# Paged attention on one core: row sums moved within the step, token sums kept across key heads, and the keys' norm applied inside Exp

## The chip, the cores and the metric

The kernel is one program on one core of one Trainium2 chip. The metric is the device time of one execution in microseconds (us), lower is better; a kernel is compared by the median of several executions. Five engines of the core work from their own queues of instructions: PE (matrix products; its weight loads are listed apart as PEld), DVE (vector work), ACT (activations and copies), POOL (vector work and gathers) and SP (which issues transfers). [...]

## What is computed

Four layers follow one another: a gated feed-forward net with low-rank adapters and a mixture of adapters (layer 0), a small adapter layer with a routed feed-forward (layer 1), paged attention with another adapter layer (layer 2), and a routed layer with a sparse adapter (layer 3). The change lies in layer 2's attention, which is, cut down (there are 8 sequences of 128 tokens here, 512 features, 32 query heads and 8 key heads of 128, and 512 cached keys per sequence):

```python
q, k, v = (einsum('bsd,ed->bse', x, W).reshape(b, s, heads, 128) for W in (Wq, Wk, Wv))
q = rope(q * rsqrt(mean(q * q) + EPS) * q_norm_w, pos)      # 32 heads
k = rope(k * rsqrt(mean(k * k) + EPS) * k_norm_w, pos)      # 8 heads
k_all = concatenate([k_cache[block_table], k])              # 512 + 128 keys
v_all = concatenate([v_cache[block_table], v])
scores = where(valid, einsum('bqhd,bkhd->bhqk', q, k_all) / sqrt(128), -1e30)
o = einsum('bhqk,bkhd->bqhd', softmax(scores), v_all)
y = einsum('bse,de->bsd', o, Wo)
```

## The kernel before, in words

The attention runs from about 300 to 1465 us of the profiled span. It is cut into 32 **steps**, `steps[n] = (qd, p)`: eight key heads `qd`, and within each four pairs `p` of sequences. Four steps with one key head are called a quarter here. Step n computes the scores, weights and mixed values of its two sequences (j = 0 and 1) for the four query heads that share the key head; the projection of step n+1 and the output product of step n-1 run within step n.

The helpers, with their lines:

- `tokens` (L910) takes the four blocks of x that a step projects (two sequences, two halves of the features) and lets `combine` (L900) form four sums and differences of them on DVE (L907, tile `xs`). They are the token side of a scheme that needs seven block products in place of eight. The blocks depend on p alone, and not on qd.
- `seven` (L915) makes those seven products on PE (L925), with copies on ACT (L933) and additions on DVE (L936, L937). It has a hook, `between`, called after the fourth product. `project` (L953) uses it for q, k and v of the next step; ACT copies one block of the result out (L973) and DVE adds and stores the other three (L968). `leave` (L1125) uses it for the output product; there DVE (L1135) and POOL (L1138, L1143) add into y.
- `rotate` (L986) multiplies q and k by the rotary tables, on POOL (L997) and DVE (L1001), while ACT sums their squares (L1008). `normed` (L1019) adds the crossed terms (L1025), takes square roots on ACT (L1023) and the reciprocal on DVE (L1026), and multiplies both q and k by it (L1029).
- `turn_cached` (L1032) transposes blocks of the gathered cache keys on DVE (L1038, tile `kt`) and sends them through memory (four writes at L1042, a read at L1045) to get keys with features on the partitions (`kT`). `turn` (L1048) transposes the new keys and q on PE (L1053, L1060).
- `weigh` (L1066) makes the scores `st`, five blocks of 128 keys by 512 queries, on PE, and ACT writes their exponentials to `pT` (L1074), with the mask as bias for the four cached blocks and a bias of 0.0 for the new keys.
- `added` (L1080) sums the five blocks of `pT` on DVE (L1085, tile `part`); `divisors` (L1088) multiplies `part` by ones on PE to add over the keys (L1094, tile `sum`), takes the reciprocal on DVE (L1100) and copies four pieces of it into `R` (L1102), which transfers spread over the partitions (L1104).
- `mix` (L1108) multiplies the weights by the values on PE (tile `av`), and DVE scales the product by `R` (L1116, tile `oT`). `outputs` (L1118) makes the four combinations of `oT` for the output product (L907, tile `os`).

`run` (L1176) lists the order of a step. A scheduler may move instructions among the engines' queues, except those that go through `kept` (L847): once the loop runs, these keep the order in which the program lists them. Most of DVE's work and `SP`'s transfers are pinned in this way; PE's products are not.

Products land in rotating buffers of the accumulator memory: a group of three with the tag `mm` (projection, output product, `sum`, transposes), three with `st`, two with `av`. A product waits until the tile that held the buffer before has been read.

In the trace of before, one step reads on PE as follows, from the output product on: `wo` products; three `st` of j = 1; one `av` block; two `st`; four `av` blocks (they finish j = 0); `sum` of j = 1; the transposes of k and q for the next step, with an `av` block of j = 1 between; five `st` of the next step's j = 0; four `av` blocks (they finish j = 1); `sum` of j = 0; the seven products of the projection; and again `wo`.

Of the kernel before, what the change touches and what calls it, by code (L numbers as in the profile page):

```python
# [28 lines left out]
NQ = 8  # L29
# [754 lines left out]
def attention(tc, a, x, ident, lens, kvrow, part, ww, wop, ypool, sums, rot, eps, psa, c2, chunks, mm):  # L784
# [59 lines left out]

    running = []

    def kept(i):  # L847
        return tc.keep_in_program_order(i) if running or i.ins.engine == pool.engine else i

    def pair(n):  # L850
        p = steps[n][1]
# [48 lines left out]
    def combine(t, a11, a12, a21, a22):  # L900
# [6 lines left out]
            kept(dve.tensor_tensor(o, l, r, op))  # L907
        return a11, a12, a22, s1, s2, s3, s4

    def tokens(n):  # L910
        b = 2 * steps[n][1]
        parts = [x[:, 2 * h : 2 * h + 2, (b + j) * P : (b + j + 1) * P] for j in range(2) for h in range(2)]
        S[n]["A"] = combine(wk.tile([P, 4, 2, P], F32, tag="xs", name=f"xs_{n}", bufs=1), *parts)

    def seven(A, B, name, u, two, out2, out4, c11, c12, c21, c22, between=lambda: None):  # L915

# [33 lines left out]
    def nothing(_):  # L950
        pass

    def project(n):  # L953

        q = wk.tile([P, 2, REP, HD], F32, tag="q", name=f"q_{n}", bufs=1)
        k = wk.tile([P, 2, 1, HD], F32, tag="k", name=f"k_{n}", bufs=1)

        def places(j, i):

            heads = q[:, j, 2 * i : 2 * i + 2, :].rearrange("p h d -> p (h d)")  # L960
            if i:
                return (heads, slice(0, HW)), (vals[n % 2 * 2 + j][:, 4, :], slice(HW, KW))
            return (heads, slice(HD, KW)), (k[:, j, 0, :], slice(0, HD))

        def put(j, i):
            def f(ps, u):
                for to, at in places(j, i):
                    dve.tensor_tensor(to, ps[:, at], u[:, at], ALU.add)  # L968
            return f

        def copied(ps):
            for to, at in places(0, 0):
                act.copy(to, ps[:, at])  # L973

        def two():
            p6 = psa.tile([P, KW], F32, tag="st", name=f"q_six_{n}", bufs=3)
            return p6, psa.tile([P, KW], F32, tag="mm", name=f"q_five_{n}", bufs=3), True

        seven(
            S[n]["A"], W[steps[n][0]].B, f"q_{n}",  # L980
            wk.tile([P, 3, KW], F32, tag="u", name=f"uq_{n}", bufs=1), two, nothing, nothing,
            copied, put(0, 1), put(1, 0), put(1, 1),
        )
        S[n].update(q=q, k=k)

# [33 lines left out]
    def normed(n):  # L1019
        s = S[n]  # L1020
        s["rest"]()
        rs = wk.tile([P, 2, REP + 1], F32, tag="rs", name=f"rs_{n}")
        kept(act.activation(rs, s["ssq"], AF.Sqrt, bias=eps, scale=1.0 / HD))  # L1023
        for r, u in (s["rk"], s["rq"]):
            kept(dve.tensor_tensor(r, r, u, ALU.add))  # L1025
        kept(dve.reciprocal(rs, rs))  # L1026
        for m, at, nh in (("k", REP, 1), ("q", 0, REP)):
            r = s["r" + m][0]
            dve.tensor_tensor(r, r, rs[:, :, at : at + nh].unsqueeze(3).to_broadcast([P, 2, nh, HD]), ALU.mult)  # L1029
# [36 lines left out]
    def weigh(n, j):  # L1066

        s = S[n]
        b = 2 * steps[n][1] + j
        pT = wk.tile([P, NC, REP, P], F32, tag="pT", name=f"pT_{n}_{j}")  # L1070
        for c in range(NC):
            ps = psa.tile([P, REP * P], F32, tag="st", name=f"st_{n}_{j}_{c}", bufs=3)
            mm(ps, s["kT"][:, c, 4 * j : 4 * j + 4, :] if c < 4 else s["kn"][:, j, :], s["qT"][j], True, True)
            act.activation(  # L1074
                pT[:, c, :, :].rearrange("p i t -> p (i t)"), ps, AF.Exp,
                bias=hide[:, b, c : c + 1] if c < 4 else 0.0,
            )
        return pT

# [81 lines left out]
    def begin():  # L1161
        weights(0)
        out_weights(0)
        gather(0, "k")
        turn_cached(0)
        gather(0, "v")
        gather(1, "k")
        W[0].factors()

    def first(n):  # L1170
        tokens(n)
        project(n)
        rotate(n)
        normed(n)

    def run(pool_, end, bank):  # L1176
# [379 lines left out]
def ending(tc, a, out, x, ident, bias3, experts, early, tile_of_w2, tile_of_aw, chunks, mm):  # L1556
# [23 lines left out]


    L3 = SimpleNamespace()
    yT = early.tile([P, DC, NT], F32, tag="yT", name="y2T")
    A2 = small("A2", [P, DC, 32], chunks(a["A2"]))
    LiT = small("LiT", [32, 8], a["LiT"])
    Li = small("Li", [8, 32], a["Li"])
# [29 lines left out]
        sp.dma_start(W["a"], chunks(a["AwT"]))  # L1616

    def turn(y2, b, bank):
        ps = bank("mm", [P, DC, P], f"y2T_{b}")
        for c in range(DC):  # L1620
            pe.transpose(ps[:, c, :], y2[:, b, c * P : (c + 1) * P], ident)
        (act.copy if b % 2 else dve.tensor_copy)(yT[:, :, b * P : (b + 1) * P], ps)

    def low(g, bank):

        ps = bank("mm", [P, P], f"z2_{g}")
        for c in range(DC):
            for j in range(HB):
                b = g * HB + j
                mmq(ps[slot(j), :], A2[:, c, :], yT[:, c, b * P : (b + 1) * P], c == 0, c == DC - 1)  # L1630
        dve.tensor_copy(zq[:, g, :], ps)

    def anchors(g, bank):
        ps = bank("mm", [P, 2, 16], f"hd_{g}")
        for i in range(2):
            t0 = (2 * g + i) * 2 * P
            for c in range(DC):
                mm(ps[:, i, :], yT[:, c, t0 + 1 : t0 + 2 * P : 2], WH[:, c, :], c == 0, c == DC - 1)
# [13 lines left out]
    def product(b, tag, bank):  # L1652

        ps = bank(tag, [P, DC, P], f"h_{b}")
        for o in range(DC):
            for c in range(DC):
                mmq(
                    ps[:, o, :], W["2"][:, c, o * P : (o + 1) * P], yT[:, c, b * P : (b + 1) * P],
                    o == 0 and c == 0, False,
                )  # L1660
        H[b] = ps
# [343 lines left out]
```

## Time and profile before

| | |
|---|---|
| three runs, median (lowest to highest) | 1640.6 us (1638.76 to 1641.55) |
| the profiled execution's own time | 1622.67 us |
| its span, first to last instruction | 1620.4 us (mean granted clock 0.990) |
| PE busy | 1568.4 us, 97% of the span |
| PE's weight loads busy | 955.7 us, 59% |
| DVE busy | 1074.9 us, 66% |
| POOL busy | 818.3 us, 50% |
| ACT busy | 564.7 us, 35% |

The profile describes one execution, in microseconds from the span's start. A group line gives a source line, an engine, an operation, what it writes and reads, its shape and count, then the busy time, the mean duration of one in nanoseconds, and the engine's idle time before the group with what ended that idle time. The timeline lists an engine's instructions in order of time: start, length, engine and line, and in square brackets the idle time before it and the releaser. The chain of work that ended last is followed back from the last instruction, at each point to whatever released it; what isn't on the chain had time to spare.

### The profile page before, as it was taken

How to read it: one execution, taken by the hardware profiler on the slowest of the kernel's cores; microseconds unless marked ns; L12 is line 12 of the kernel's file. 1: busy time of each engine (PE TensorE's matmuls, PEld its weight loads, DVE VectorE, ACT ScalarE, POOL GpSimd, SP SyncE). 2: the span in 40 equal slices, each digit the busy share in tenths (PEclk: the TensorE clock that was granted, in tenths of full speed). 3: DMA queues.
4: the chain of work that ended last, by engine and by line, in shares of the span. 5: the costliest groups of instructions: out<-in, count | busy, mean ns of one | idle time of the engine just before them, and what ended most of it. 6: DMA issues, size and time to landing. Idle time of an engine off the chain costs nothing.

```text
span 1620.4 us, 19220 instructions
## 1 busy us (share of the span) xinstructions
PE 1568.4 (97%) x6305; PEld 955.7 (59%) x6305; DVE 1074.9 (66%) x2235; ACT 564.7 (35%) x1390; POOL 818.3 (50%) x778
## 2 busy tenths in 40 slices
PE   9999998979999999999999999999999999999998
PEld 7888884445555555555555555555555555559653
DVE  4575523477878787787878777787787877743141
ACT  1111110244445544444544444544444553420210
POOL 1341107254666676666667666666765676710000
PEclk9999998999999999999999999999999999999899
DMA  9110003031323323232332223323232332311000
GB/s 299 38 41 23 1 1 103 34 116 53 111 67 102 116 69 100 68 111 75 102 106 75 94 74 104 90 88 110 71 99 71 111 100 65 122 31 64 0 20 35
DMA packets 92237, 127.98 MB, mean 79 GB/s; under 512 B 19360, under 2 KB 59488, under 8 KB 92000
## 3 DMA queue, kind: packets, MB, share of 16 engines
q1 hardware_dynamic: 73984, 89.65, 17.9%
q0 software_dynamic: 17056, 36.49, 7.5%
q8 instruction: 52, 0.85, 0.2%
q10 hardware_dynamic: 1088, 0.52, 0.1%
q14 instruction: 57, 0.47, 0.1%
HBM read 92.91 MB, written 21.10 MB: 70 GB/s over the span
## 4 chain that ended last, share of the span: by engine, by line
PE 77%; DVE 15%; POOL 3%; DMA 2%; issue 2%; ACT 1%; SPq 0%; ACTq 0%; DVEq 0%; POOLq 0%
PE st L53 10%; PE av L53 10%; PE q_six L925 8%; PE g L362 7%; PE q_one L925 5%; PE q_five L925 5%; PE wo_two L925 5%; PE dn L362 4%; DVE part L1085 4%; PE wo_one L925 3%; PE wo_six L925 3%; DVE rq L1025 3%; DVE xs L907 2%; PE z L53 2%; PE h L1574 2%
## 5 line engine op out<-in xcount | busy, mean ns | idle before, releaser
L893 POOL DMA_INDIRECT vals<-in_v_cache,kvrow_v x256 | 273.1, 1067 | 73.2 <-issue 52.1
L893 POOL DMA_INDIRECT kn<-in_k_cache,kvrow_k x256 | 267.0, 1043 | 79.9 <-issue 77.6
L53 PE MATMUL av<-pT,vals 128*128 128x512 f32 x640 | 296.2, 594 | 0.0
L53 PE MATMUL st<-qT,kT 128*128 128x512 f32 x512 | 239.1, 599 | 4.3 <-DMA kT<-turned 4.3
L53 PEld LDWEIGHTS av<-pT,vals 128*128 128x128 f32 x640 | 119.4, 191 | 137.8 <-issue 135.6
L1074 ACT ACTIVATE pT<-st,hide 128x512 f32<-128x512 f32 x256 | 169.5, 687 | 46.6 <-PE st L53 43.9
L997 POOL TENSOR_TENSOR vq<-q,txq 128x512 f32<-128x512 f32 x64 | 83.5, 1326 | 161.2 <-DVE q L968 161.2
L53 PEld LDWEIGHTS st<-qT,kT 128*128 128x128 f32 x512 | 93.6, 192 | 99.4 <-issue 80.0
L1085 DVE TENSOR_TENSOR part<-pT 128x512 f32<-128x512 f32 x128 | 85.5, 692 | 68.6 <-ACT pT L1074 68.6
L1143 POOL TENSOR_TENSOR y<-y,uo 128x512 f32<-128x512 f32 x32 | 44.1, 1379 | 115.3 <-DVE y L1135 115.3
L1062 ACT COPY qT<-qTp 128x512 f32<-128x512 f32 x64 | 37.5, 586 | 169.2 <-PE qTp L1060 169.2
L925 PE MATMUL q_one<-q,x 128*128 128x384 f32 x256 | 96.2, 498 | 0.0
L925 PE MATMUL q_six<-q_s,xs 128*128 128x384 f32 x256 | 94.3, 486 | 0.0
L1008 ACT ACTIVATE sqq<-q 128x128 f32<-128x128 f32 x256 | 79.4, 310 | 8.3 <-DVE q L968 1.5
L1116 DVE TENSOR_TENSOR oT<-av,R 128x512 f32<-128x512 f32 x64 | 44.1, 688 | 42.5 <-PE av L53 39.1
L1025 DVE TENSOR_TENSOR rq<-rq,vq 128x1024 f32<-128x1024 f32 x32 | 70.4, 2200 | 1.2 <-POOL vq L997 1.2
L925 PEld LDWEIGHTS q_six<-q_s,xs 128*128 128x128 f32 x256 | 48.6, 190 | 36.1 <-issue 4.0
L1102 DVE COPY R<-r 32x128 f32<-32x128 f32 x256 | 66.1, 258 | 3.7
L925 PE MATMUL wo_one<-o,oT 128*128 128x256 f32 x256 | 65.8, 379 | 0.0
L933 ACT COPY uq<-q_one 128x384 f32<-128x384 f32 x32 | 15.3, 479 | 144.0 <-PE q_one L925 144.0
L53 PE MATMUL st<-qT,kTs 128*128 128x512 f32 x128 | 65.5, 593 | 0.0
L925 PEld LDWEIGHTS q_one<-q,x 128*128 128x128 f32 x256 | 46.0, 189 | 31.4 <-issue 6.0
(391 smaller groups left out, 2883.5 us busy)
## 6 DMA issues: line engine op xcount, KB each, us to landing
turned<-kt SPq DMA_DIRECT2D x128, 128.0 KB
kT<-turned SPq DMA_DIRECT2D x32, 512.0 KB
R<-R SPq DMA_DIRECT2D x192, 64.0 KB
q<-in_WqT SPq DMA_DIRECT2D x8, 1024.0 KB
o<-in_WoT SPq DMA_DIRECT2D x8, 1024.0 KB
kn<-in_k_cache,kvrow_k POOLq DMA_INDIRECT x256, 2.6
vals<-in_v_cache,kvrow_v POOLq DMA_INDIRECT x256, 2.7
wd<-in_WdT SPq DMA_DIRECT2D x2, 1280.0 KB
```

The source lines that it names most:

```text
L53: pe.matmul(o, lhsT, rhs, start=start, stop=stop)
L362: pe.matmul(o, lhsT, rhs, start=start, stop=stop, skip_group_check=True)
L893: kept(pool.indirect_dma_start(out=d[:, c, :], out_offset=None, in_=kc if what == "k" else vc, in_offset=bass.IndirectOffsetOnAxis(ap=kvro ...
L925: pe.matmul(o, l[:, c, :], r[:, c, :], start=start and c == 0, stop=c == 1, skip_group_check=True)
L997: kept(pool.tensor_tensor(u[:, :, :, lo : lo + 64], t[:, :, :, hi : hi + 64], wx[:, :, lo : lo + 64].unsqueeze(2).to_broadcast(part_), ALU ...
L1008: kept(act.activation(sq, t[:, j, i, :], AF.Square, accum_out=ssq[:, j, at + i : at + i + 1]))
L1025: kept(dve.tensor_tensor(r, r, u, ALU.add))
L1074: act.activation(pT[:, c, :, :].rearrange("p i t -> p (i t)"), ps, AF.Exp, bias=hide[:, b, c : c + 1] if c < 4 else 0.0,)
L1085: kept(dve.tensor_tensor(o, l, r, ALU.add))
L1102: kept(dve.tensor_copy(R[0:32, i * P : (i + 1) * P], r[32 * i : 32 * i + 32, :]))
L1116: kept(dve.tensor_tensor(S[n]["oT"][:, j].rearrange("p i t -> p (i t)"), ps, S[n]["R", j], ALU.mult))
L1143: kept(pool.tensor_tensor(t, t, u.unsqueeze(1).to_broadcast([P, 2, HW]), ALU.add))
```

## The change

Six things are edited.

1. **The row sums move.** `divisors(n, 0)` is called no longer right after `mix(n - 1, 1)` but through the hook `between` of the next step's projection. `divisors(n - 1, 1)` is called no longer at the end of its own step but in the next one, after the scores of j = 0.
2. **Token sums are kept.** For the key heads 1 to 6, `xs` of a pair p is computed once, in a tile that all of them share; heads 0 and 7 compute theirs anew as before. The shared tile takes the place that the last stage's transposed y (`y2T`) uses later, and `y2T` is therefore allocated when it is first written.
3. **The new keys are not multiplied by their norm.** The multiplication of k at L1029 is gone; the reciprocal root, one number for each key, becomes the scale of the Exp of the fifth block, where keys lie on the partitions.
4. **The turn of the cached keys moves** behind the output product and its additions, on DVE and on SP. Its DVE transposes are now always pinned.
5. **In `normed`** the additions are listed ahead of the square root, and the multiplication of q is pinned.
6. **At the start** `turn_cached(0)` moves from `begin` to behind the projection of step 0.

Built, the changed kernel has 47 rows of `xs` work on DVE in place of 127, and the 32 multiplications of k are gone. PE's order in a middle step is now: `wo` products; three `st` of j = 1; one `av` block; two `st`; four `av` blocks; the transposes; one `av` block of j = 1; **`sum` of j = 1**; three `av` blocks; five `st` of the next j = 0; the last `av` block; five of the projection's products and half of the sixth; **`sum` of j = 0**; the rest of the projection; and again `wo`. The `sum` of j = 0 takes over the buffer of the projection's first product (`q_one`). On DVE the reciprocal and the four copies of j = 0 stand among the projection's additions; the `kt` transposes stand after the last addition into y and ahead of the additions of the crossed terms.

```diff
-    def kept(i):
-        return tc.keep_in_program_order(i) if running or i.ins.engine == pool.engine else i
+    def kept(i, always=False):
+        return tc.keep_in_program_order(i) if always or running or i.ins.engine == pool.engine else i
...
+    kept_sums = {}
+
     def tokens(n):
-        b = 2 * steps[n][1]
+        qd, p = steps[n]
+        b = 2 * p
+        if 0 < qd < NQ - 1 and p in kept_sums:
+            S[n]["A"] = kept_sums[p]
+            return
         parts = [x[:, 2 * h : 2 * h + 2, (b + j) * P : (b + j + 1) * P] for j in range(2) for h in range(2)]
-        S[n]["A"] = combine(wk.tile([P, 4, 2, P], F32, tag="xs", name=f"xs_{n}", bufs=1), *parts)
+        if 0 < qd < NQ - 1:
+            if not kept_sums:
+                late.append(late[0].tile([P, NP, 4, 2, P], F32, tag="yT", name="xs_all"))
+            S[n]["A"] = kept_sums[p] = combine(late[1][:, p], *parts)
+        else:
+            S[n]["A"] = combine(wk.tile([P, 4, 2, P], F32, tag="xs", name=f"xs_{n}", bufs=1), *parts)
...
-    def project(n):
+    def project(n, between=lambda: None):
...
-            copied, put(0, 1), put(1, 0), put(1, 1),
+            copied, put(0, 1), put(1, 0), put(1, 1), between,
...
         rs = wk.tile([P, 2, REP + 1], F32, tag="rs", name=f"rs_{n}")
+        for m in "kq":
+            r, u = s["r" + m]
+            kept(dve.tensor_tensor(r, r, u, ALU.add))
+            s[m] = r
         kept(act.activation(rs, s["ssq"], AF.Sqrt, bias=eps, scale=1.0 / HD))
-        for r, u in (s["rk"], s["rq"]):
-            kept(dve.tensor_tensor(r, r, u, ALU.add))
         kept(dve.reciprocal(rs, rs))
-        for m, at, nh in (("k", REP, 1), ("q", 0, REP)):
-            r = s["r" + m][0]
-            dve.tensor_tensor(r, r, rs[:, :, at : at + nh].unsqueeze(3).to_broadcast([P, 2, nh, HD]), ALU.mult)
-            s[m] = r
+        full = [P, 2, REP, HD]
+        kept(dve.tensor_tensor(s["q"], s["q"], rs[:, :, 0:REP].unsqueeze(3).to_broadcast(full), ALU.mult))
+        s["rs"] = rs
...
             kept(dve.transpose(
                 t[:, :, 4 * j : 4 * j + 4, :], s["kc"][j].rearrange("p c (b d) -> p b c d", b=4)
-            ))
+            ), True)
...
                 pT[:, c, :, :].rearrange("p i t -> p (i t)"), ps, AF.Exp,
-                bias=hide[:, b, c : c + 1] if c < 4 else 0.0,
+                **(
+                    dict(bias=hide[:, b, c : c + 1]) if c < 4
+                    else dict(bias=0.0, scale=s["rs"][:, j, REP : REP + 1])
+                ),
...
         gather(0, "k")
-        turn_cached(0)
         gather(0, "v")
...
         project(n)
+        if n == 0:
+            turn_cached(n)
         rotate(n)
...
             pT = weigh(n, 0)
+            if last:
+                divisors(n - 1, 1)
             added(n, 0, pT)
             if last:
                 mix(n - 1, 1, last)
-            divisors(n, 0)
-            if last:
                 outputs(n - 1)
             if after:
-                project(after)
+                project(after, lambda: divisors(n, 0))
+                leave(n - 1, lambda: rotate(after))
+            else:
+                divisors(n, 0)
             if n + 1 < len(steps):
                 turn_cached(n + 1)
-            if after:
-                leave(n - 1, lambda: rotate(after))
-            elif last:
+            if last and not after:
                 leave(n - 1)
...
             mix(n, 0, pT)
-            divisors(n, 1)
             if n + 1 < len(steps):
                 turn(n + 1)
...
+        divisors(n, 1)
         mix(n, 1, last)
         outputs(n)
```

The remaining hunks replace the name of the last stage's `yT` by the tile allocated at its first use.

More of the change, by code (lines that the diff above doesn't have):

```diff
@@ L1582, in ending @@
     L3 = SimpleNamespace()
-    yT = early.tile([P, DC, NT], F32, tag="yT", name="y2T")
+    Y2T = []
     A2 = small("A2", [P, DC, 32], chunks(a["A2"]))
@@ L1618, in turn @@
     def turn(y2, b, bank):
+        if not Y2T:
+            Y2T.append(early.tile([P, DC, NT], F32, tag="yT", name="y2T"))
         ps = bank("mm", [P, DC, P], f"y2T_{b}")
@@ L1621, in turn @@
             pe.transpose(ps[:, c, :], y2[:, b, c * P : (c + 1) * P], ident)
-        (act.copy if b % 2 else dve.tensor_copy)(yT[:, :, b * P : (b + 1) * P], ps)
+        (act.copy if b % 2 else dve.tensor_copy)(Y2T[0][:, :, b * P : (b + 1) * P], ps)
     def low(g, bank):
@@ L1629, in low @@
                 b = g * HB + j
-                mmq(ps[slot(j), :], A2[:, c, :], yT[:, c, b * P : (b + 1) * P], c == 0, c == DC - 1)
+                mmq(ps[slot(j), :], A2[:, c, :], Y2T[0][:, c, b * P : (b + 1) * P], c == 0, c == DC - 1)
         dve.tensor_copy(zq[:, g, :], ps)
@@ L1637, in anchors @@
             for c in range(DC):
-                mm(ps[:, i, :], yT[:, c, t0 + 1 : t0 + 2 * P : 2], WH[:, c, :], c == 0, c == DC - 1)
+                mm(ps[:, i, :], Y2T[0][:, c, t0 + 1 : t0 + 2 * P : 2], WH[:, c, :], c == 0, c == DC - 1)
         dve.tensor_tensor(
@@ L1657, in product @@
                 mmq(
-                    ps[:, o, :], W["2"][:, c, o * P : (o + 1) * P], yT[:, c, b * P : (b + 1) * P],
+                    ps[:, o, :], W["2"][:, c, o * P : (o + 1) * P], Y2T[0][:, c, b * P : (b + 1) * P],
                     o == 0 and c == 0, False,
```

## The prediction, with its working

> **What bounds the kernel now.** I read the page first, then PE's waits, then the chain in order of time, then the timeline of one step. In the page, PE is busy nearly throughout, but DVE holds 15% of the chain:
>
> ```profile
> PE 1568.4 (97%) x6305; PEld 955.7 (59%) x6305; DVE 1074.9 (66%) x2235; ACT 564.7 (35%) x1390; POOL 818.3 (50%) x778
> PE 77%; DVE 15%; POOL 3%; DMA 2%; issue 2%; ACT 1%; SPq 0%; ACTq 0%; DVEq 0%; POOLq 0%
> ```
>
> Since no product is removed, only PE's waits can be won. Their list (us in total, times, longest) names what the change can touch:
>
> ```profile
> PE sum L1094 <- DVE part L1085: 19.2, 23, 2.6
> ...
> PE st L53 <- DMA kT<-turned: 4.3, 1, 4.3
> PE y2T L1621 <- POOL y L1143: 3.7, 2, 2.9
> PE eo_l L53 <- DVE x L300: 2.6, 1, 2.6
> ```
>
> The chain in one step shows how `sum` comes to wait: for about 10 us DVE alone carries it, from the crossed terms through k's and q's norm and the token sums to the sums of `pT`.
>
> ```profile
> 805.19 0.88 PE wo_six L925 x4
> 806.85 2.21 DVE rq L1025
> 809.22 0.70 DVE rk L1029
> 809.92 1.13 DVE rq L1029
> 811.43 1.10 DVE xs L907 x3
> 812.52 1.21 DVE part L1085 x2
> 813.76 0.70 DVE part L1085
> 814.56 0.70 DVE part L1085
> 816.53 0.86 PE av L53 x2
> ```
>
> The same view gives the step length as the distance between its rows of ten `st`: 35.17 us, but 34.43 from 538.00 to 572.43, the one step in four whose `xs` are not in this place.
>
> ```profile
> 502.83 4.29 PE st L53 x10
> 538.00 4.29 PE st L53 x10
> 572.43 4.29 PE st L53 x10
> 607.60 4.29 PE st L53 x10
> ```
>
> So the late `part` costs 0.74 us in three of four steps, and nothing in the fourth. In PE's timeline the pause ahead of `sum` in this step is 0.67 us.
>
> [...] the crossed-term addition of q, which lies beside POOL's additions into y (806.60 to 809.64 in its timeline), takes 2200 ns in the mean, the multiplication of the same size right after 1213 ns[...]. [...] Exp with the mask as bias takes 687 ns, with a constant 597 ns. [...] The trace has half-clock stretches of 3.41 us right after pauses of 4.3 us (at 363) and 2.6 us (at 1342).
>
> **The change part by part.** All sums are made against the profiled execution's own time, 1622.7 us (1620.4 span, 2.3 around it); the median of the runs is 1.0110 times that. Let S be the start of the first `st` of j = 1 (805.89 in the step shown) and T the start of `q_one`.
>
> *`sum` of j = 1 goes behind one more `av` block, k's norm and most `xs` go away.* Behind S, PE now has five `st` and five `av` blocks of 0.86 us, the transposes (0.28, 0.44, 0.44) and an `av` block (0.86): `sum` comes up at S + 10.6. On DVE, the last addition into y ends at S + 0.6; two `kt` transposes of 0.69 us follow, in place of nothing; then the additions of k (0.41) and q. POOL's additions into y end at S + 3.7 in the trace, so I let the contended addition end at S + 4.2, the reciprocal (0.20) and the multiplication of q (1.21) at S + 5.7, four `part` additions (2.75) at S + 8.5; with `xs` (1.5) at S + 10. Both are ahead of S + 10.6: the wait goes. [...] Of PE's 23 waits two are 2.6 and 1.7 us; one of 1.5 lies at 395, where weights are prepared on DVE; the other 20 are 0.67 to 0.74. Gain: 20 x 0.74 = 14.8, and 1.5 at 395. The removed DVE work, some 33 us of `xs` (80 x 417 ns) and 21.8 us of k's norm (32 x 681 ns), is worth nothing beyond these waits. Bounds: 10 to 17 together.
>
> *The norm as Exp's scale* makes 64 activations some 90 ns longer. PE's `st` and ACT's Exp run in turn at 0.86 us and 0.69: it is hidden. If ACT were late, 64 x 0.09 = 5.8 us is the most.
>
> *`sum` of j = 0 within the projection.* Its order needs the buffer of `q_one`, which ACT's two copies release. Before:
>
> ```profile
> 832.43 1.45 PE L925 MATMUL q_five<-q,xs 128*128 128x384 f32 x4
> 832.63 0.37 ACT L973 COPY q<-q_one 128x256 f32<-128x256 f32 x1 [4.64 <-PE q_one L925]
> 832.90 0.27 ACT L973 COPY k<-q_one 128x128 f32<-128x128 f32 x1
> ```
>
> The copies end at 833.17, or 0.74 after the fifth product begins; half of that product takes 0.65. With 0.06 for the semaphore (the reciprocal starts 0.08 after `sum` ends at 815.72) PE waits 0.15 in each of 29 steps: +4.4 (0 to 8.7, if it is none or twice that).
>
> On DVE, the reciprocal (0.95) and the four copies now stand ahead of the last additions of the projection:
>
> ```profile
> 826.24 0.95 DVE L1100 RECIPROCAL r<-sum 128x128 f32<-128x128 f32 x1
> 827.22 1.15 DVE L1102 COPY R<-r 32x128 f32<-32x128 f32 x4
> ```
>
> Five products of 1.29 (the first 0.1 more) and half of the sixth take until T + 7.2, so `sum` runs from T + 7.34 to 7.76, the reciprocal to 8.8, the addition of `q_five` to 9.2, the copies to 10.2, the addition that stores v to 10.4. `wo_one` can take the buffer of `sum`, free at 8.8. `wo_two` needs the one of `q_five`, at T + 10.6: 0.2 us to spare, cost nothing. The addition of `q_six` follows at 10.4 to 11.2, 0.4 to 0.6 us later against the output product than before, and POOL's rotary products with it; the crossed terms need them only at S + 2.3, some 2 us after they were ready before. `R`'s transfers get about 10 us more than before.
>
> *The turn of cached keys* leaves DVE's idle time. On SP its four writes (1.9 us of issue at 837.07) and read follow 5.8 us later; at 835.75 to 845 the way from the transposes to `kT` took 9 us beside weight transfers, so it lands at S + 10 at worst, and `st` needs it at S + 12. R's transfers stand ahead of it on SP and are long issued. Cost 0; 1 us a step if it were 3 us slower.
>
> *Late steps.* Of the 2.6 us at 1342, where POOL has an extra addition, I leave half, as the same chain on DVE is shortened by 2.2 and lengthened by 1.4; without a pause that long, the half-clock stretch behind it, worth 1.0, should go: -2.3 (0 to -3.6). The wait of `y2T` for POOL stays. At the end `sum` of the last j = 1 comes after the last Exp: +0.5.
>
> *Start.* The additions of x no longer stand behind q's crossed terms (-1.8 of 2.6); the projection now fills the wait for `kT` of step 1 (-4.3, and -1.6 for its half clock); against that, `sum` of step 0 waits some 3.6 in place of 1.7 and may bring a half-clock stretch (+1.9, +1.7), and the first `kT`, now queued on SP behind the 2 MB that are moved from 329 to 334, lands at about 335 to 336, when `st` needs it (336.34): +1.1. Together -3 (-6 to +3).
>
> Sum: -14.8 - 1.5 - 2.3 - 3.0 + 4.4 + 0.5 = -16.7, so 1606.0 in the profiled execution; times 1.0110, **1623.7**.
>
> **Rivals.** *Slower: DVE's queue inside the projection.* The reciprocal and copies, 2.1 us, stand ahead of the additions that free `wo_two`'s buffer, with 0.2 us to spare. If they run later than I have them, each step waits anew. Without the slot's 4.4 the gain is 21.1, so 0.73 us in 29 steps eats it all; at 1.0 us the profiled time is 1622.7 - 21.1 + 29 = 1630.6, or 1648.6. For it: the copies of one step can take 1.15 together, and everything after them is in one queue. Against: POOL is idle from 831.4 to 835.8[...].
> *Half the gain:* [...] -8, or 1632.5. Against it stands the 2 us of room in steps without `xs`.
> *More gain:* the slot's wait is hidden and the half-clock stretches at the start and at 1342 vanish: -14.8 - 1.5 - 3.6 - 6 + 0.5 = -25.4, or 1614.9.
> *The moves cancel:* waits merely go over to other products, within 0.2%.
>
> **Numbers.** As described 0.60 (own range 1618 to 1630), more gain 0.13, half the gain 0.12, no change 0.04, slower 0.11. A measurement can tell about 0.2% (3.3 us) from no change. Hence faster 0.85, same 0.04, slower 0.11. The range leaves out the slower case and the tail of the strong one: 1611 to 1637.
>
> **What would show it.** Right: steps of 34.4 to 34.7 us throughout; PE's wait `sum` on `part` under 4 us in all; `sum` of j = 0 waiting about 0.15 for ACT's copies; `wo_two` not waiting for DVE; the fifth Exp near 690 ns; no wait for `kT` at 363. Wrong: a new wait of `wo_two` or `rq`'s chain in each step; `kT` on the list with many entries; steps above 35.2.

## The result, and the profile after

The changed kernel took 1686.97 us in the median of four runs (1677.89 to 1693.08), the kernel before 1641.07 us (1638.76 to 1642.21) beside it: a ratio of 1.0277, with a 95% interval of 1.0229 to 1.0325. The forecast was 1623.7, faster.

The runs that followed fell on five chips, on two of which the kernel before took about 1624 us and on three 1644 to 1700 us, so each ratio below compares kernels on one chip, and the chip is named (that of this first result is not recorded).

The profiled execution of the changed kernel took 1686.06 us (span 1683.9, mean granted clock 0.979). Its page, with the row of busy times and the chain's shares by engine:

```profile
PE 1589.4 (94%) x6305; PEld 962.6 (57%) x6305; DVE 1012.7 (60%) x2123; ACT 565.7 (34%) x1388; POOL 798.6 (47%) x778
PE 85%; issue 3%; DVE 3%; DMA 2%; POOL 2%; another core or an unknown queue 2%; ACT 1%; SPq 0%; ACTq 0%; DVEq 0%; POOLq 0%
```

DVE's share of the chain fell from 15% to 3%, as the change intends, and yet the span is 63.5 us longer than in the profile of before. One entry has no place in a program on a single core: 2% of the chain were released by "another core or an unknown queue". PE's waits (us in total, times, longest):

```profile
PE q_five L938 <- DVE uq L950: 18.4, 10, 8.6
PE st L53 <- ACT pT L1089: 16.7, 3, 8.3
PE q_one L938 <- ACT uq L946: 14.9, 5, 3.1
PE sum L1112 <- ACT k L986: 13.6, 14, 1.3
PE y2T L1643 <- POOL y L1161: 3.8, 2, 3.0
PE sum L1112 <- DVE part L1103: 3.2, 2, 2.7
```

`sum` on `part`, 19.2 us before, is down to 3.2. Four waits have come up, and they are irregular: `q_five` waits 10 times among some 30 steps, `st` 3 times but for up to 8.3 us. The chain's rows of ten `st` show the same scatter:

```profile
541.54 4.29 PE st L53 x10
...
577.16 4.29 PE st L53 x10
...
613.00 4.29 PE st L53 x10
...
649.37 4.29 PE st L53 x10
```

These steps are 35.62, 35.84 and 36.37 us long; one, from 948.68 to 989.21, takes 40.53. In the profile of before, and in that of `after_fifth` below, the steps of the middle repeat in groups of four; here they do not.

One such wait, read in the timeline of all engines in the changed kernel (start, length, engine and line, and in brackets the idle time before it):

```profile
1068.20 1.45 PE L938 MATMUL q_five<-q_s,xs_all 128*128 128x384 f32 x4
...
1069.07 0.48 ACT L946 COPY uq<-q_one 128x384 f32<-128x384 f32 x1 [3.42 <-PE q_six L938]
...
1070.49 0.56 DVE L949 TENSOR_TENSOR uq<-q_six,uq 128x384 f32<-128x384 f32 x1 [1.21 <-PE q_five L938]
...
1070.66 0.94 POOL L893 DMA_INDIRECT kn<-in_k_cache,kvrow_k  x1 [0.30 <-issue]
1070.78 1.45 PE L938 MATMUL q_one<-q,x 128*128 128x384 f32 x4
1073.25 0.56 DVE L950 TENSOR_TENSOR uq<-q_five,uq 128x384 f32<-128x384 f32 x1 [2.20 <-PE q_one L938]
...
1073.86 0.91 PE L938 MATMUL q_five<-q,xs_all 128*128 128x384 f32 x2 [1.63 <-DVE uq L950]
```

The addition at L950 needs the product `q_five`, which ended at 1069.65, and the addition at L949, which ended at 1071.05. It starts at 1073.25, when no work that it needs is left, and PE stands for 1.63 us. What is late is PE's semaphore update: between 1070.40 and 1073.23 PE's semaphore has no record, although products with an update ended at 1070.94 and 1072.23 too. Until 1071.60, when the last one ends, POOL issues gathers.

### The profile page after: what moved, and what is told of

It reads as the page before. It is cut to its first block, busy times and chain, and to the rows that moved or that the text cites. A ratio compares the mean times of both kernels' runs of the same rounds, so it can differ in the third digit from the quotient of the medians.

```text
span 1683.9 us, 19213 instructions
## 1 busy us (share of the span) xinstructions
PE 1589.4 (94%) x6305; PEld 962.6 (57%) x6305; DVE 1012.7 (60%) x2123; ACT 565.7 (34%) x1388; POOL 798.6 (47%) x778
## 3 DMA queue, kind: packets, MB, share of 16 engines
q1 hardware_dynamic: 73984, 89.65, 17.6%
q0 software_dynamic: 17056, 36.49, 7.2%
HBM read 92.91 MB, written 21.10 MB: 68 GB/s over the span
## 4 chain that ended last, share of the span: by engine, by line
PE 85%; issue 3%; DVE 3%; DMA 2%; POOL 2%; another core or an unknown queue 2%; ACT 1%; SPq 0%; ACTq 0%; DVEq 0%; POOLq 0%
PE av L53 16%; PE st L53 15%; PE g L362 7%; PE q_six L938 7%; PE q_one L938 6%; PE q_five L938 5%; PE wo_two L938 5%; PE dn L362 4%; PE wo_one L938 3%; PE wo_six L938 3%; PE z L53 2%; PE h L1594 2%; PE o L53 2%; PE sum L1112 2%
## 5 line engine op out<-in xcount | busy, mean ns | idle before, releaser
L893 POOL DMA_INDIRECT vals<-in_v_cache,kvrow_v x256 | 283.3, 1107 | 73.3 <-issue 51.8
L893 POOL DMA_INDIRECT kn<-in_k_cache,kvrow_k x256 | 262.3, 1025 | 97.9 <-issue 76.1
L53 PE MATMUL av<-pT,vals 128*128 128x512 f32 x640 | 303.7, 601 | 0.0
L53 PE MATMUL st<-qT,kT 128*128 128x512 f32 x512 | 239.4, 598 | 16.7 <-ACT pT L1089 16.7
L1118 DVE RECIPROCAL r<-sum 128x128 f32<-128x128 f32 x64 | 61.2, 956 | 62.3 <-PE sum L1112 49.5
L938 PE MATMUL q_six<-q_s,xs_all 128*128 128x384 f32 x192 | 69.8, 486 | 0.0
L1120 DVE COPY R<-r 32x128 f32<-32x128 f32 x256 | 59.8, 234 | 3.7
L938 PE MATMUL wo_two<-o_s,os 128*128 128x256 f32 x256 | 60.6, 380 | 0.4 <-DVE vals L981 0.4
L986 ACT COPY q<-q_one 128x256 f32<-128x256 f32 x32 | 11.9, 373 | 145.8 <-PE q_one L938 136.9
```

The lines of the kernel that those rows point to most:

```text
L53: pe.matmul(o, lhsT, rhs, start=start, stop=stop)
L893: kept(pool.indirect_dma_start(out=d[:, c, :], out_offset=None, in_=kc if what == "k" else vc, in_offset=bass.IndirectOffsetOnAxis(ap=kvro ...
L938: pe.matmul(o, l[:, c, :], r[:, c, :], start=start and c == 0, stop=c == 1, skip_group_check=True)
L1118: kept(dve.reciprocal(r, ps))
L1120: kept(dve.tensor_copy(R[0:32, i * P : (i + 1) * P], r[32 * i : 32 * i + 32, :]))
```

## The experiments

Two theories were set against each other. *Parts*: one of the edits makes the new waits. *Late updates*: in some runs the semaphore updates of PE, ACT and DVE come late while POOL's gathers run; then it is a condition that the run meets, and the changed order merely pays more for it. To tell them apart in a trace, I counted for each engine the updates that have no record of their own within 0.12 us after the end of the instruction that makes them (late, or not recorded; these are called not prompt).

### Which part, and does the result repeat

The changed kernel unaltered (`same_again`), and the kernel before with one part each: kept token sums alone (`b_tokens`), row sums moved alone (`b_divs`), the turn of cached keys moved alone (`b_turn`).

```diff
# b_tokens
+        if 0 < qd < NQ - 1 and p in kept_sums:
+            S[n]["A"] = kept_sums[p]
+            return
# b_divs
+            if last:
+                divisors(n - 1, 1)
...
-                project(after)
+                project(after, lambda: divisors(n, 0))
...
-            divisors(n, 1)
# b_turn
-        turn_cached(0)
...
+            if n + 1 < len(steps):
+                turn_cached(n + 1)
```

> The changed kernel itself, unchanged, in a new load beside the kernel before. Theory A (semaphore updates of PE, ACT and DVE come late while POOL's gathers run, and the program's order brings that on): again about 1.02 to 1.03 times the kernel before, with 20 or more late updates in each step. Theory B (the late updates belong to one load or one session of the chip and not to the program): no late updates, and then what was predicted without them, about 0.99. Theory C (the row sum inside the projection simply waits for ACT's copies and DVE's queue, nothing is late): again 1.02 to 1.03, but with updates prompt, which the trace of the first run already speaks against.

> The kernel before with the kept token sums alone. All theories: in steps of the key heads 2 to 6 the 80 additions are gone from DVE and the wait of the row sum of j = 1 (0.74 us in three of four steps) goes with them, so some 10 to 15 us faster, ratio 0.991 to 0.994. Theory A, if the kept sums or the shared tile bring on the late updates: slower, 1.01 to 1.03, with late updates during the gathers.

> The kernel before with the two moves of the row sums alone. My working: the wait on part goes in 20 steps (-15 us), the slot of q_one costs 0.15 in 29 (+4), so 0.992 to 0.996 if updates are prompt. Theory C or theory A with the row sums as the cause: 1.01 to 1.03, in A with late updates during the gathers, in C without.

> The kernel before with the turn of the cached keys moved behind the output product, and at the start, alone. My working: 1.4 us more on DVE's chain ahead of part, so 1.4 us more waiting in some 28 steps at worst: 1.00 to 1.025, with prompt updates; theory A with this move as the cause: late updates during the gathers and ACT and DVE waiting for products long done.

Measured, all on chip 15 (before 1643.82 us): `same_again` 1690.77, ratio 1.0286 [1.0253, 1.0319]; `b_tokens` 1663.67, 1.0135 [1.0083, 1.0188]; `b_divs` 1716.76, 1.0445 [1.0409, 1.0481]; `b_turn` 1698.88, 1.0320 [1.0287, 1.0352]. So the slowdown repeats. `b_divs` lies above all that was expected for it, and every part that was tried alone is slower, even the kept sums, which only take away work of DVE and place the sums elsewhere. The parts do not add up either: 1.4, 4.5 and 3.2% make 9.0, all edits together 2.9%. That speaks against one guilty part. In all four traces several hundred updates are not prompt (the table below; `same_again` has 298 of DVE and 142 of ACT), and in the profile of before sixteen.

### The same before on another chip, and without gathers

`before_again` is the kernel before. `b_hw` and `a_hw` are the kernels before and after with the attention's gathers replaced by plain transfers that SP issues; they read fixed rows of the cache instead of those that the block table chooses, so their keys and values are other ones, of the same amount.

```diff
-                kept(pool.indirect_dma_start(
-                    out=d[:, c, :], out_offset=None, in_=kc if what == "k" else vc,
-                    in_offset=bass.IndirectOffsetOnAxis(ap=kvrow[what][:, qd, i : i + 1], axis=0),
-                ))
+            g0 = (2 * p + j) * 512 + qd * 64
+            src = (kc if what == "k" else vc)[g0 : g0 + 512, :].rearrange("(c p) d -> p c d", p=P)
+            kept(sp.dma_start(d[:, 0:4, :], src))
```

> The kernel before, unchanged, with a new profile. If late semaphore updates belong to the conditions of these timed runs and not to the change, this profile shows them too, during POOL's gathers, in about the number of the changed kernel (20 to 30 in a step), and the waits they bring add up to the 18 us between the profiled execution of the first page (1622.7) and the timed runs (1641). If they belong to the change, this profile is free of them as the first one was.

> The kernel before with the 512 indirect gathers of keys and values on POOL replaced by 128 plain transfers issued by SP, of rows that the block table does not choose (so the attention reads other keys and values). If late updates come with POOL's gathers, none is left and the time falls to about the span of the first page, 1620 to 1625, or ratio 0.985 to 0.99. If they come from something else, 1635 to 1650 with late updates.

> The changed kernel with the same replacement of the gathers. If my sum was right but for late updates, then with prompt updates this is 10 to 20 us faster than the kernel before with the replacement, 1600 to 1612, ratio 0.975 to 0.983. If the order of the change is at fault by itself (the row sum waiting for ACT's copies, DVE's queue in the projection), it stays slower than that kernel by 20 to 45 us: 1645 to 1670.

Measured on chip 1 (before 1623.58 us in the median of 23 runs): `before_again` 1623.26, ratio 1.0003 [0.9995, 1.0012]; `b_hw` 1611.07, 0.9929 [0.9910, 0.9948]; `a_hw` 1592.73, 0.9823 [0.9807, 0.9840]. Two things follow. The kernel before, which took 1641 to 1644 us elsewhere, takes 1624 here, so its first profile (1622.67) was no sample of the 1640.6 that stood beside it. And without gathers the change brings 18.3 us (1611.07 to 1592.73), about the 16.7 of the forecast. Both kernels came out below their ranges (1620 to 1625 and 1600 to 1612), because the replacement itself brings 12.5 us where updates are prompt (1623.58 to 1611.07), which no expectation had.

### The changed kernel and the row sums on a third chip

No edit (`after_third`), and the same edit as `b_divs` (`b_divs_second`).

> The changed kernel, unchanged, once more, since the kernel before took 1641 to 1644 us where updates were late and 1623 where they were prompt. Where the kernel before is at 1622 to 1625 here: theory A' (the change is worth what was worked out, and late updates during gathers turn it round) gives 1602 to 1610, ratio 0.987 to 0.992, with at most a handful of late updates. Theory D (the change by itself brings late updates) gives 1660 to 1695 with 20 or more late updates in a step. Where the kernel before is at 1640 or more: about 1688, as twice already.

> The two moves of the row sums alone, which cost 4.5% with late updates. With prompt updates: 20 waits on part of 0.74 go, 29 of 0.15 come, so 1610 to 1616, ratio 0.992 to 0.996. With late updates: 1710 to 1722 again.

Measured on chip 13 (before 1643.55 us): 1683.71, ratio 1.0268 [1.0224, 1.0312], and 1716.35, 1.0451 [1.0394, 1.0508]. Updates were late again (the table below), so this tells only that the result repeats on a further chip, for both kernels within 0.2%.

### A slow before, and the changed kernel without gathers beside it

No edit (`before_third`, `after_fourth`), and the edit of `a_hw` again (`a_hw_second`).

> The kernel before with a profile beside the changed one. Where it takes 1640 us or more I expect late updates during the gathers in this profile too (20 or more in a step), and fewer PE waits from them than in the changed kernel: some 18 us in all. Where it takes 1623, none.

> The changed kernel once more. Where the kernel before takes 1623 here: 1602 to 1610, ratio 0.987 to 0.992, updates prompt. Where it takes 1640 or more: 1680 to 1692, ratio 1.024 to 1.032, updates late. A time of 1680 beside 1623, or of 1605 beside 1641, would sink the theory that late updates decide the sign.

> The changed kernel with plain transfers by SP in place of the indirect gathers (it reads rows that the block table does not choose). If late updates come only while POOL gathers, this kernel has none here, whatever the kernel before takes, and stays at 1592 to 1597; beside a kernel before of 1643 that is a ratio of 0.97. If the condition makes updates late without gathers as well, it is 1620 or more.

Measured on chip 2 (before 1700.25 us): `before_third` 1699.13, ratio 0.9987 [0.9969, 1.0005]; `after_fourth` 1731.78, 1.0169 [1.0110, 1.0228]; `a_hw_second` 1593.50, 0.9365 [0.9315, 0.9416]. The expected sizes were missed: the kernel before was to lose some 18 us to late updates, and the changed one was to take 1680 to 1692. The last run is the strongest single result: on the chip where the kernel before loses 76 us, the changed kernel without the attention's gathers takes 1593.50, on chip 1 it took 1592.73. The condition was there in this execution: six gathers at the start of the program remain in it (6.3 to 15.1 us), and during these, or within 0.4 us behind them, seven updates of DVE are not prompt, against none in `a_hw` on chip 1. After them there is none on DVE or ACT. So the loss goes with the gathers. The amount of data is no cause: the page's queue rows of `a_hw_second` show the bytes moved from POOL's queue to SP's.

```profile
q1 hardware_dynamic: 141568, 123.21, 26.9%
q0 software_dynamic: 672, 2.90, 0.5%
HBM read 92.91 MB, written 21.10 MB: 72 GB/s over the span
```

Those of `after` have 73984 packets and 89.65 MB in q1, 17056 and 36.49 MB in q0, and the same 92.91 MB read. What it is in the gathers that goes with late updates is not shown, since POOL's time and the queue change with them.

`before_third` gave the profile of a slow before. Its PE waits:

```profile
PE q_six L925 <- DVE r L1100: 29.7, 8, 4.1
PE sum L1094 <- DVE part L1085: 19.2, 23, 2.6
PE q_five L925 <- DVE uq L937: 18.7, 14, 1.9
```

The middle row is the one of the first profile, unchanged; the two around it are new, and no line of code differs.

### The changed kernel where updates are prompt, and a mended order

No edit (`after_fifth`). `a_early` moves two of the value gathers in between POOL's rotary products and its additions into y, and one addition into y from POOL to DVE, so that a step's gathers end about 4 us earlier; if late updates cost because gathers reach into the projection, this should help where they are late.

```diff
-            kept(pool.tensor_tensor(y(1, 1), u, y(1, 1), ALU.add))
+            kept(dve.tensor_tensor(y(1, 1), u, y(1, 1), ALU.add))
...
-                leave(n - 1, lambda: rotate(after))
+                leave(n - 1, lambda: (rotate(after), gather(after, "v", range(2))))
...
-                    gather(after, "v")
+                    gather(after, "v", range(2, 8))
```

> The changed kernel beside the kernel before. Where the kernel before takes 1621 to 1626 (updates prompt): 1602 to 1610, ratio 0.987 to 0.992, if late updates alone turned my sum round; over 1640 if the order of the change is slow by itself with gathers on POOL. Where it takes 1640 or more: 1.015 to 1.03, updates late.

> The changed kernel with POOL's gathers ended some 4 us earlier in each step: two gathers of values go between POOL's rotary products and its additions into y, where POOL idles 2.5 us, and one of the two additions into y goes from POOL to DVE. The gathers then end about T + 2, where T is the start of the projection, in place of T + 6. If late updates cost what they meet in the projection, most of the waits for ACT's and DVE's uq go: with late updates 1620 to 1655, beside 1680 to 1732 of the changed kernel; with prompt updates within 3 us of the changed kernel. If the gathers' end does not matter, within 1% of the changed kernel in both conditions.

Measured on chip 9 (before 1624.26 us): `after_fifth` 1605.65, ratio 0.9884 [0.9868, 0.9901]; `a_early` 1607.67, 0.9908 [0.9886, 0.9930]. The very kernel that was 2.8% slower is 1.2% faster here. Page of `after_fifth`, the same two rows as above, and its first PE waits:

```profile
PE 1566.3 (98%) x6305; PEld 959.1 (60%) x6305; DVE 1008.3 (63%) x2123; ACT 565.3 (35%) x1388; POOL 796.8 (50%) x778
PE 89%; DVE 4%; issue 3%; POOL 2%; DMA 1%; ACT 0%; ACTq 0%; DVEq 0%; POOLq 0%
```

```profile
PE q_five L938 <- DVE uq L950: 8.5, 1, 8.5
PE sum L1112 <- DVE part L1103: 4.1, 3, 2.7
PE y2T L1643 <- POOL y L1161: 3.8, 2, 3.0
```

No unknown queue in the chain, and one wait of `q_five` in place of ten. The same place in a step as the one shown above, in the timeline of `after_fifth`, with gathers running as they did there:

```profile
821.98 1.45 PE L938 MATMUL q_five<-q_s,xs_all 128*128 128x384 f32 x4
...
822.99 0.54 DVE L949 TENSOR_TENSOR uq<-q_six,uq 128x384 f32<-128x384 f32 x1
823.19 0.94 POOL L893 DMA_INDIRECT kn<-in_k_cache,kvrow_k  x1 [0.30 <-issue]
823.27 1.45 PE L938 MATMUL q_six<-q_s,xs_all 128*128 128x384 f32 x4
823.64 0.56 DVE L950 TENSOR_TENSOR uq<-q_five,uq 128x384 f32<-128x384 f32 x1
...
825.85 0.81 PE L938 MATMUL q_five<-q,xs_all 128*128 128x384 f32 x2
```

From the start of `q_five` to that of L950 it is 1.66 us here (821.98 to 823.64), and 5.05 us in the slow trace (1068.20 to 1073.25). So gathers alone do not make this delay; gathers do in the condition that was met on certain chips. Whether it belongs to the chip or to the session was not separated: chip 2 alone was met twice, late both times.

### The mended order where updates are late

The edits of `a_early` (`a_early_second`) and of `b_divs` (`b_divs_third`), and the changed kernel (`after_sixth`), on one chip.

> The changed kernel with POOL's gathers ended about 4 us earlier in each step. With prompt updates it took 1607.7 beside 1605.7 and told nothing of late ones. With late updates (kernel before at 1640 or more): if the projection's chain between PE, ACT and DVE pays for them, at least a third of the loss goes, 1.00 to 1.015 of the kernel before; if the payer is elsewhere (the scores, whose buffers ACT frees), as slow as the changed kernel.

> The changed kernel on the same chip, to compare a_early with: 1603 to 1607 with prompt updates, 1.015 to 1.03 of the kernel before with late ones.

> The two moves of the row sums alone. With prompt updates, never tried yet: the waits on part go (-15), the slot's wait comes (+4), 1610 to 1616. With late updates: 1.04 to 1.05 as twice before, and then the row sum in the projection is the dearest part under late updates.

Measured on chip 2 (before 1699.84 us): `a_early_second` 1850.96, ratio 1.0883 [1.0842, 1.0923]; `after_sixth` 1724.50, 1.0141 [1.0110, 1.0172]; `b_divs_third` 1732.23, 1.0185 [1.0143, 1.0226]. The expectation for `a_early_second` failed badly: this order, whose gathers end earlier in the step, made the loss larger, not smaller. `b_divs_third` missed its 1.04 to 1.05 as well, so the row sum in the projection is not the dearest part on every chip. In `a_early_second` the waits are now at the scores, in most steps:

```profile
PE st L53 <- ACT pT L1091: 159.0, 26, 7.5
```

One of the 26, in the timeline of `a_early_second`:

```profile
863.95 2.74 PE L53 MATMUL st<-qT,kT 128*128 128x512 f32 x6
...
869.19 0.94 POOL L895 DMA_INDIRECT kn<-in_k_cache,kvrow_k  x1 [0.30 <-issue]
871.06 0.69 ACT L1091 ACTIVATE pT<-st,hide 128x512 f32<-128x512 f32 x1 [11.00 <-remote]
...
871.80 1.22 PE L53 MATMUL st<-qT,kT 128*128 128x512 f32 x1 [5.11 <-issue]
```

Six products fill the three buffers of `st` until 866.69, the first two of them by about 865. The first Exp starts only at 871.06, when the last gather has ended at 870.13; the profile can't name its releaser ("remote"). PE, with all three buffers of `st` full, takes up its next product at 871.80, after 5.11 us. What ends such a delay is not shown. In the first example two further products with an update ended, at 1070.94 and 1072.23, and L950 still started only at 1073.25, after the last gather's end at 1071.60. And the changed kernel's gathers run under these scores too (1049.85 to 1071.60 around scores that start at 1060.47), with 3 such waits in its trace and not 26; why, stays open, and the two edits of `a_early` were not tried apart.

### The count of updates

Updates that were not prompt, PE / DVE / ACT, of some 1320 to 1490, 1770 to 1870 and 1000 in a trace (PE's count changes by up to twenty with the way in which records are paired with instructions):

| kernel, chip | not prompt | median us |
|---|---|---|
| before (first profile) | 13 / 3 / 0 | 1622.67 (that execution) |
| `before_again`, 1 | 11 / 4 / 0 | 1623.26 |
| `after_fifth`, 9 | 13 / 0 / 0 | 1605.65 |
| `a_early`, 9 | 13 / 0 / 0 | 1607.67 |
| `b_hw`, 1 | 13 / 0 / 0 | 1611.07 |
| `a_hw`, 1 | 13 / 0 / 0 | 1592.73 |
| `a_hw_second`, 2 | 13 / 7 / 0 | 1593.50 |
| `before_third`, 2 | 327 / 322 / 146 | 1699.13 |
| after (the result) | 400 / 298 / 140 | 1686.97 |
| `after_third`, 13 | 380 / 284 / 140 | 1683.71 |
| `after_fourth`, 2 | 430 / 266 / 134 | 1731.78 |
| `after_sixth`, 2 | 425 / 287 / 148 | 1724.50 |
| `b_tokens`, 15 | 352 / 278 / 145 | 1663.67 |
| `b_divs`, 15 | 325 / 276 / 107 | 1716.76 |
| `b_turn`, 15 | 376 / 261 / 133 | 1698.88 |
| `same_again`, 15 | 402 / 298 / 142 | 1690.77 |
| `b_divs_second`, 13 | 336 / 255 / 105 | 1716.35 |
| `b_divs_third`, 2 | 316 / 264 / 94 | 1732.23 |
| `a_early_second`, 2 | 378 / 291 / 89 | 1850.96 |

There is nothing between 13 and 316 for PE, and the 11 to 13 of the upper half come 0.121 to 0.122 us after the end, just outside the limit. The count has no gradation; the price that a kernel pays has, and the count does not tell it (`before_third` and `a_early_second` differ by 150 us at nearly the same count). In every trace of the lower half but `b_divs_second`, one to six updates of DVE are not prompt already around the first six gathers, from 6.5 to 16 us, some 240 us before the attention's own gathers begin; in those of the upper half there are none there, except the seven of `a_hw_second`. Of the 438 updates of DVE and ACT that are not prompt in the changed kernel's profile, 426 fall into a run of gathers (pauses of up to 0.44 us counted in), where only 41% of these engines' updates lie. In the changed kernel's profile 23 to 32 of some 60 updates in a middle step's batch of sixteen gathers are not prompt, and the last of them lies within 1 us of the end of the batch's last gather in nearly all batches (for the batch shown, gathers until 1071.60, last such update 1072.23).

## Why the prediction was wrong, point by point

**The step that failed: "the median of the runs is 1.0110 times that".** I took the 18 us between the profiled execution and the timed runs for a scale that both kernels share. The runs show two conditions in its place: 1623 to 1624 us for the kernel before where updates are prompt, 1641 to 1644 or 1700 where they are late. The first profile was a prompt execution beside late runs. The cost of late updates belongs to an order of work and does not multiply. For the result: the kernel before pays 1641.07 - 1623.6 = 17.5 us, the changed one 1686.97 - 1605.65 = 81.3; their difference of 63.9, less the 18.0 that the change gains where updates are prompt (1623.6 - 1605.65), is the 45.9 measured. That sum only restates the medians; what shows the condition behind it are the counts and the runs without gathers. No rival had this in it; all four changed waits that a prompt profile shows. The slower one, nearest in time with 1648.6, named a wait of `wo_two` for DVE in each step; the changed kernel's profile has one such wait, of 0.4 us.

Where the 81.3 lie can be read from the pages. In the profiled executions the changed kernel is 79.0 us longer than `after_fifth`. PE's busy time is 23.1 longer (1589.4 against 1566.3, at a granted clock of 0.979 against 0.990). Of the other 56, the four waits that have come up give 63.6, less the 9.9 that `q_five` (8.5) and `st` (1.4) have in `after_fifth` too: 53.7.

**The steps of the sum, where updates are prompt.** `after_fifth` took 1607.05 us in its profiled execution; 1606.0 was forecast for it.

*`sum` of j = 1 on `part`, -14.8, and -1.5 at 395: right.* The wait fell from 19.2 in 23 to 4.1 in 3. The chain of one step in `after_fifth` shows `sum` between two `av` pieces without a gap:

```profile
810.43 0.86 PE av L53 x2
811.29 0.36 PE sum L1112 x8
811.64 2.77 PE av L53 x6
```

The working behind it holds too: in the step whose first `st` of j = 1 starts at S = 835.09, the timeline has the addition of q, which overlaps POOL's into y there, end at S + 4.0 (forecast S + 4.2) and the multiplication of q at S + 5.3 (S + 5.7).

*`sum` of j = 0, +4.4: mis-sized.* It waits 0.15 us, as I had it, but before it had already waited 0.09, which I did not take off: some 0.07 in each step, about +2. The 27 middle steps together brought 14.8 us against the 11.9 of the three terms so far. Four steps take 137.98 us in `after_fifth` (504.81 to 642.79 on the chain), 139.94 before (502.83 to 642.77). The rows of ten `st` between them are:

```profile
504.81 4.29 PE st L53 x10
...
538.45 4.29 PE st L53 x10
...
572.95 4.29 PE st L53 x10
...
607.44 4.29 PE st L53 x10
```

They make 34.50 us in the mean. One distance of four is 33.64 and one 35.35, since once in a quarter PE's order shifts by one `av` piece; there is no wait in it.

*The norm as Exp's scale, 0: right.* The fifth Exp takes 687 ns in place of 597, and no product waits for it:

```profile
L1089 ACT ACTIVATE pT<-st,rs 128x512 f32<-128x512 f32 x64 | 44.0, 687 | 14.2 <-PE st L53 14.2
```

*DVE's queue in the projection, 0, and the turn in the loop, 0: right.* Neither `wo_two` nor `kT` is among PE's waits in `after_fifth`.

*Late steps and end, -2.3 and +0.5: 1.3 us too little.* Measured are -2.3 for the last four steps, and -0.75 behind them.

*The start, -3.0 (-6 to +3): wrong, within its bounds.* Measured from 250 us on it is +0.35. Two effects were missed, and they nearly cancel. Up to 310, 7.5 us are won: the transposes of the first cached keys had stood in DVE's queue, waiting for their gather (6.37 us before the one at 263.64, 3.65 before the one at 268.84, in the profile of before), ahead of work that PE needed. After that 7.9 are lost, by this path in the timeline of `after_fifth`:

```profile
315.21 0.95 POOL L893 DMA_INDIRECT kn<-in_k_cache,kvrow_k  x1 [18.32 <-DVE kt L1053]
...
327.73 1.47 DVE L1038 TENSOR_TENSOR rq<-rq,vq 128x1024 f32<-128x1024 f32 x1 [7.74 <-POOL vq L1010]
...
332.27 2.93 PE L938 MATMUL q_five<-q,xs 128*128 128x384 f32 x4 [8.53 <-DVE uq L950]
```

The gathers of step 1's keys need the buffer that the moved transposes release; they stand ahead of the rotary products in POOL's queue, and so the delay goes on to DVE and PE. My text named what the turn was moved past on SP's queue, and not what waits for its buffer on POOL's.

Together: -14.8 in the middle steps, -3.05 late, +0.35 at the start, and +2.0 before 250 us, where no edit lies and the two executions merely differ, make the -15.5 by which the span of `after_fifth` (1604.9) is under that of before (1620.4); -16.7 was forecast.

So the order of work came out as forecast, and the sum within 1.1 us, for the condition in which the profile of before had been taken. That the sum is so close is in part luck: terms that are off by -2.9 (middle), -1.25 (late), +3.35 (start) and +2.0 (before 250 us) nearly cancel.

**What stays open.** Why updates are late on some chips and not on others, whether that belongs to the chip or to the session, and which update is held, no run shows. The replacement of the gathers changes their kind, the engine that issues them and POOL's load together, so which of these matters was not tried apart. There is no profile of the kernel before on chips 13 and 15, where it loses some 20 us and not 76, so that the size of its loss is explained for chip 2 alone. The parts were each tried where updates are late only; how much each brings where they are prompt was not measured. No order with gathers was found that is safe in both conditions: `a_early` was meant as one and is the worst. Whether to keep the change depends on the chip: ratio 0.9884 where updates are prompt, 1.0141 to 1.0286 where they are late.

## What to carry to other kernels

When the profiled execution and the timed runs of the same kernel differ by more than their scatter, find the reason before turning one into the other: here the 1.1% between them was a condition that the profile did not contain. Where PE waits for an answer from ACT or DVE with a buffer or two to spare, while POOL issues gathers, an order that is tight in a prompt trace can be the slower one (here its ratio was 0.9884 where updates are prompt and 1.0141 to 1.0286 where they are late); look for "remote", "an unknown queue" and steps of unequal length. And of work that is moved, follow the buffer that it releases as well as the queue that it leaves.

## What the runs showed of the hardware

- On three of five chips (one of them met in two sessions, the others in one), semaphore updates of PE, ACT and DVE came late or left no record while POOL's gathers ran: 316 to 430 of some 1485 on PE, against 11 to 13 (in the changed kernel's profile PE's semaphore has 1261 records for 1488 updates). In `a_early_second` an Exp started about 6 us after the products that it reads had ended (865 to 871 above). With the attention's gathers replaced, the changed kernel took 1592.73 and 1593.50 us on a chip of either kind.
- DVE's crossed-term addition of q took longer where it began beside an addition of POOL into y. It takes 1208 ns at the least. In `after_fifth` the one from 837.31 begins 0.65 us before POOL's addition into y ends (837.96) and takes 0.53 us beyond the least. In the profile of before, the one from 806.76 begins 1.22 us before the end of the POOL addition that runs when it begins (807.98) and takes 1.08 beyond it. In the profiles of the kernels before and after, in every step where it begins beside such an addition (29 of 32 and 27 of 32), the excess is that overlap less 0.12 to 0.14 us. This was read from traces, and no run was made to test it.
